# Attention times values as twenty block products, with half of the turned blocks going through DRAM

## The chip, the cores and the metric

The kernel runs on one core of one Trainium2 chip. The metric is the device time of one execution in microseconds; less is better. Everything is float32. A matmul in float32 is two TensorE instructions in the profile (a transpose on TensorE is one).

Names: PE is TensorE's matmul, PEld its weight load, DVE is VectorE, ACT ScalarE, POOL GpSimd, SP SyncE, which issues nearly all DMAs from one queue in order. Every engine runs its own instructions strictly in order; an instruction that waits holds up all behind it on that engine.

## The reference, cut to what matters

```python
B, L, S, D = 8, 100, 361, 512        # batches, queries, keys, width
H, K, F = 16, 128, 2048              # heads, width of a head, width of the MLP

def layer0(x, ctx):                  # one head, width 512, residual with factor alpha
    q, k, v = x @ wq.T, ctx @ wk.T, ctx @ wv.T
    return x + alpha * (softmax(q @ k.T / sqrt(512)) @ v) @ wo.T

def cross_attention(h, ctx):         # run twice, with weights of their own
    qh = (h @ wq + bq).reshape(B, L, H, K)
    kh = concat((ctx @ wk + bk).reshape(B, S, H, K), bias_k)   # one more key
    vh = concat((ctx @ wv + bv).reshape(B, S, H, K), bias_v)   # one more value
    p = softmax(einsum('bqhk,bthk->bhqt', qh, kh) / sqrt(K))
    return einsum('bhqt,bthk->bqhk', p, vh).reshape(B, L, H * K) @ wo + bo

x = layer0(x, ctx)
x = x + cross_attention(layer_norm(x), ctx)   # layer 1 of the two large ones
x = x + cross_attention(layer_norm(x), ctx)   # layer 2
x = x + gelu(layer_norm(x) @ w_fc1 + b_fc1) @ w_fc2 + b_fc2
```

## The kernel before, in words

The kernel never forms keys or values. A head's query is multiplied by `wk` transposed (the "wide query", 512 numbers), so that scores are wide query times context, and the probabilities are multiplied with the raw context first (the "mix", again 512 numbers per head and query) and with `wv` afterwards. Wide queries and mixes live in one tile `Z` of [128, 4, 2, 1600]: 4 chunks of the width 512, 2 batches, 16 x 100 rows (head, query).

The two attention layers are walked in steps (layer l, pair of batches q, head group g), 2 x 4 x 3 = 24 of them, each with two batches j: 48 tiles. `ROWS` gives the rows of a head group: 576, 512 and 512. They are scored in pairs of 128-row tiles (`PAIRS`), and in group 0 in one tile of 64 rows besides (`lone_tile`, `LONE`). For a pair:

- `pair_sums` (GpSimd) and `pair_part` form the scores in four parts by a product scheme with seven block products in place of eight (x, y, z in PSUM, evicted by ScalarE and VectorE); `pair_exps` and `normalise` make probabilities `p` of [128 rows, 361 keys and one bias key].
- `rows_turned` and `turned` put keys on partitions: VectorE transposes 32x32 blocks (L359). One instruction takes 32 rows x 192 numbers, for one quarter of the keys: 16 instructions for a pair of tiles, 8 smaller ones for the lone tile. They are placed 30 places behind in the scheduler's priority (`TURN_BEHIND`).
- the result is `pT`, a tile of nine blocks of [128, 288 or 256]: three key chunks (128, 128, 105 and the bias key) times two halves of the columns, and three places for sums. After the last quarter `column_sums` sends the bias key's row to DRAM (`pbd`) and forms four sums on GpSimd (L822 to L825).
- `mixed` (L843 on) multiplies the context's blocks with these: for each of two halves m of the width, four parts with 11 products of [128 or 105] x 128 x [288 or 256], accumulated in PSUM with evictions in between (L867, L870, L875 and L889 on ScalarE; L878, L884 and L885 on VectorE). Its result overwrites the tile's columns of `Z`. A next product into the same accumulation must wait for the eviction of the last.

The context's blocks come by `fill_ctx` in five loads per batch: three from the input, two from `cxd`, a DRAM tile that `ctx_sums` filled in layer 0 with five sums per batch (GpSimd, L442 to L446).

The order is written out by hand: the mix of a tile runs beside the scoring of the next tile, among the projections of the next step (`queries`, `wide_queries`) and the output products of the last one (`head_out`); `woven` and `apart` mix these lists, and `apart` keeps units with the same `chunks_of` from standing next to each other. A scheduler then orders instructions on each engine. Weights come by SP into rings of buffers (`W_SLOTS` 6, `V_SLOTS` 2, `C_SLOTS` 2 for the context); a load waits on SP until its buffer is free. PSUM has eight buffers for all uses.

Layer 0 comes first, one batch after the other: transposed context (`ctx_transposed`), scores, probabilities, mix, `ctx_sums`, output. Batches alternate between two rings for the raw context (`ctx0`, and `ctx` of [128, 2560]).

Of the kernel before, what the change touches and what calls it, by code (L numbers as in the profile page):

```python
# [19 lines left out]
P = 128  # L20
# [3 lines left out]
QB = 2  # L24
# [8 lines left out]
PAIRS = ((64, 320), (576, 832), (1088, 1344))  # L33
# [3 lines left out]
GWIDTH = 576  # L37

# [5 lines left out]
A11, A12, A22, A13, A23, A33, M1, M2, M3, M4 = range(10)  # L44
# [36 lines left out]
def two_cross_attentions(ctx: ExitStack, tc: tile.TileContext, a: dict, out: bass.AP):  # L81
# [16 lines left out]
    cxd = [dram.tile([P, 10 * P], F32, tag=f"cxd{b}", name=f"cxd{b}") for b in range(B)]  # L98
# [60 lines left out]
    def fill_ctx0(key, t):  # L159
        src = a["ctx_2048"][key[2]]  # L160
        t = t[:, : 3 * D].rearrange("p (k n) -> p k n", k=3)
        nc.sync.dma_start(out=t[:, :2, :], in_=src[: 2 * P].rearrange("(c p) n -> p c n", p=P))
        nc.sync.dma_start(out=t[:TS, 2, :], in_=src[2 * P :])

    def fill_ctx(key, t):
        if key[1] < 0:
            return fill_ctx0(key, t)
        src = a["ctx_2048"][key[2]]
        t = t.rearrange("p (m u n) -> p m u n", m=2, n=P)
        nc.sync.dma_start(out=t[:, :, A11, :], in_=src[:P].rearrange("p (m n) -> p m n", m=2)[:, :, :P])  # L170
        nc.sync.dma_start(
            out=t[:, :, A12:A13, :], in_=src[P : 2 * P].rearrange("p (m u n) -> p m u n", m=2, n=P)
        )
        nc.sync.dma_start(
            out=t[:TS, :, A13:A33, :], in_=src[2 * P :].rearrange("p (m u n) -> p m u n", m=2, n=P)
        )
        d = cxd[key[2]].rearrange("p (m u n) -> p m u n", m=2, n=P)
        nc.sync.dma_start(out=t[:, :, M1:, :], in_=d[:, :, 1:, :])
        nc.sync.dma_start(out=t[:TS, :, A33, :], in_=d[:TS, :, 0, :])
# [165 lines left out]
    def transposed(name, p, rows, dst):  # L345
# [4 lines left out]
        evacuate(dst, pt[:, :, :rows])  # L350

    def turned(p, dst, tiles, rows, quarter):

        keys = slice(quarter * QD, (quarter + 1) * QD)
        src = p[:, :tiles, :].rearrange("p m (k j b) -> p m k j b", k=3, b=QD)
        dst = dst.rearrange("p k (m i a) -> p m k i a", m=tiles, a=QD)
        with tc.high_priority(offset=-TURN_BEHIND):
            for i in range(rows // QD):
                nc.vector.transpose(dst[keys, :, :, i, :], src[i * QD : (i + 1) * QD, :, :, quarter, :])  # L359


# [76 lines left out]
    def ctx_sums(b):  # L438

        cx = ctx0(b).rearrange("p k (m u n) -> p k m u n", m=2, n=P)  # L440
        t = work.tile([P, 2, 5, P], F32, tag="pb", name=f"msum_{b}", bufs=1)
        nc.gpsimd.tensor_tensor(t[:, :, 1], cx[:, 0, :, 1], cx[:, 1, :, 1], ALU.add)  # L442
        nc.gpsimd.tensor_tensor(t[:, :, 2], t[:, :, 1], cx[:, 0, :, 0], ALU.subtract)
        nc.gpsimd.tensor_tensor(t[:, :, 3], cx[:, 0, :, 1], cx[:, 0, :, 0], ALU.subtract)
        nc.gpsimd.tensor_tensor(t[:, :, 4], cx[:, 1, :, 0], t[:, :, 2], ALU.subtract)
        nc.gpsimd.tensor_tensor(t[:TS, :, 0], cx[:TS, 2, :, 0], cx[:TS, 2, :, 1], ALU.subtract)  # L446
        out = cxd[b].rearrange("p (m u n) -> p m u n", m=2, n=P)
        tc.keep_in_program_order(nc.sync.dma_start(out=out[:, :, 1:, :], in_=t[:, :, 1:, :]))
        nc.sync.dma_start(out=out[:TS, :, 0, :], in_=t[:TS, :, 0, :])
# [78 lines left out]
    def layer0_units():  # L528
# [21 lines left out]
        for b in range(B):  # L550
            res.append(unit(lambda b=b: l0_probs(b)))
            res += scored(b + 1)
            res.append(unit(lambda b=b: l0_mixed(b), key0("ctx", b)))
            res.append(unit(lambda b=b: ctx_sums(b), key0("ctx", b)))
            res += turned(b + 2) + normed0(b + 1)
            res += weights(b + 4)
            if b == 0:
# [866 lines left out]
```

## Time and profile before

| what | us |
|---|---|
| median of three runs (lowest, highest) | 1986.92 (1986.24, 1991.32) |
| the profiled execution, its own time | 1987.13 |
| its span in the trace | 1985.3 |
| TensorE matmuls busy | 1942.6 |
| VectorE busy | 1279.1 |
| ScalarE busy | 761.3 |
| GpSimd busy | 699.8 |
| VectorE's transposes L359, 1664 of them | 602.2 |
| TensorE's mix L858, 2112 instructions | mean 391 (x), 390 (z), 388 (y) ns each |
| granted TensorE clock | 0.998 |

A span is what lies between the first and the last instruction in the trace; the execution's own time has the launch around it. The busy time of a group counts the time in which at least one of its instructions was under way; matmuls overlap each other, so the mean of one is longer than the distance between two. "Idle before" is the time that an engine stood still just ahead of a group, with what ended it. A wait on an engine that is not needed at that moment costs nothing.

### The profile page before, as it was taken

How to read it: one execution, taken by the hardware profiler on the slowest of the kernel's cores; microseconds unless marked ns; L12 is line 12 of the kernel's file. 1: busy time of each engine (PE TensorE's matmuls, PEld its weight loads, DVE VectorE, ACT ScalarE, POOL GpSimd, SP SyncE). 2: the span in 40 equal slices, each digit the busy share in tenths (PEclk: the TensorE clock that was granted, in tenths of full speed). 3: DMA queues.
4: the chain of work that ended last, by engine and by line, in shares of the span. 5: the costliest groups of instructions: out<-in, count | busy, mean ns of one | idle time of the engine just before them, and what ended most of it. 6: DMA issues, size and time to landing. Idle time of an engine off the chain costs nothing.

```text
span 1985.3 us, 31528 instructions
## 1 busy us (share of the span) xinstructions
PE 1942.6 (98%) x10991; PEld 1788.5 (90%) x10991; DVE 1279.1 (64%) x3555; ACT 761.3 (38%) x2018; POOL 699.8 (35%) x1147
## 2 busy tenths in 40 slices
PE   9999999999999999999999999999999999999999
PEld 5668899999999899999989898999999999889998
DVE  2464776667677677676765766676667677765553
ACT  0324544444442344344433344444433444421331
POOL 3232433543344144525243323333243243325140
PEclk9999999999999999999999999999999999999999
DMA  7696323742545356616533453234234442136432
GB/s 256 243 314 219 99 83 118 243 138 67 189 159 168 108 144 224 206 55 188 173 109 127 120 176 108 86 89 169 89 122 132 128 131 81 58 87 192 125 122 76
DMA packets 250683, 283.90 MB, mean 143 GB/s; under 512 B 37608, under 2 KB 212108, under 8 KB 247196
## 3 DMA queue, kind: packets, MB, share of 16 engines
q1 hardware_dynamic: 246340, 271.51, 43.1%
q0 software_dynamic: 2112, 6.40, 0.9%
q10 hardware_dynamic: 2072, 3.97, 0.6%
q8 instruction: 88, 1.44, 0.3%
q14 instruction: 71, 0.58, 0.1%
HBM read 242.86 MB, written 38.97 MB: 142 GB/s over the span
## 4 chain that ended last, share of the span: by engine, by line
PE 83%; DVE 10%; ACT 3%; DMA 2%; issue 1%; POOL 0%; SPq 0%; DVEq 0%; ACTq 0%
PE sx L748 10%; PE mx L858 9%; PE pq L672 8%; PE mz L858 7%; PE pwo_P L971 7%; PE po L908 7%; PE pqw L688 7%; DVE pT L359 5%; PE sz L748 5%; PE my L858 4%; PE sy L748 2%; PE pgx L1062 2%; PE pfx L1111 2%; PE pfz L1111 1%; PE pgz L1062 1%
## 5 line engine op out<-in xcount | busy, mean ns | idle before, releaser
L359 DVE STREAM_TRANSPOSE pT<-p 32x192 f32<-32x192 f32 (+1 forms) x1664 | 602.2, 362 | 90.9 <-ACT p L343 63.2
L858 PE MATMUL mx<-pT,ctx 128*128 128x256 f32 (+3 forms) x960 | 280.1, 391 | 8.2 <-DVE Z L884 3.1
L748 PE MATMUL sx<-cT,Z 128*128 128x181 f32 x1152 | 225.7, 317 | 2.1 <-DVE p L788 2.1
L782 POOL TENSOR_SCALAR p<-nsb 128x1 f32<-128x1 f32 x192 | 38.1, 217 | 499.1 <-DVE pT L359 441.2
L858 PE MATMUL mz<-pT,ctx 105*128 105x256 f32 (+3 forms) x768 | 206.1, 390 | 7.5 <-ACT Z L870 4.1
L748 PEld LDWEIGHTS sx<-cT,Z 128*128 128x128 f32 x1152 | 193.2, 190 | 13.7 <-DVE p L788 3.6
L672 PE MATMUL pq<-hT,wq 128*128 128x200 f32 x1024 | 194.5, 335 | 2.2 <-DMA wq<-in_L_xattn_wq_dram 2.2
L688 PE MATMUL pqw<-q,wkT 128*128 128x200 f32 x1024 | 194.4, 333 | 0.6 <-ACT q L680 0.6
L908 PE MATMUL po<-Z,wv 128*128 128x200 f32 x1024 | 194.8, 335 | 0.0
L858 PEld LDWEIGHTS mx<-pT,ctx 128*128 128x128 f32 (+1 forms) x960 | 169.4, 189 | 24.9 <-DVE Z L884 7.1
L802 ACT ACTIVATE p<-p,nm 128x362 f32<-128x362 f32 x192 | 114.7, 597 | 179.9 <-DVE nm L801 176.6
L672 PEld LDWEIGHTS pq<-hT,wq 128*128 128x128 f32 x1024 | 177.3, 191 | 6.9 <-issue 3.2
L688 PEld LDWEIGHTS pqw<-q,wkT 128*128 128x128 f32 x1024 | 176.2, 189 | 7.1 <-ACT q L680 1.4
L908 PEld LDWEIGHTS po<-Z,wv 128*128 128x128 f32 x1024 | 176.2, 191 | 5.0 <-issue 1.0
L858 PEld LDWEIGHTS mz<-pT,ctx 128*128 128x128 f32 (+1 forms) x768 | 144.2, 190 | 40.2 <-ACT Z L870 8.2
L801 DVE TENSOR_REDUCE nm<-p 128x1 f32<-128x362 f32 x192 | 101.5, 529 | 112.4 <-ACT p L793 102.7
L731 POOL TENSOR_TENSOR sums<-Z 128x256 f32<-128x256 f32 x96 | 70.8, 737 | 229.7 <-ACT Z L691 135.5
L691 ACT COPY Z<-pqw 128x400 f32<-128x400 f32 x256 | 122.4, 489 | 73.8 <-PE pqw L688 73.3
L748 PE MATMUL sz<-cT,sums 128*128 128x181 f32 x768 | 149.5, 316 | 0.0
L343 ACT ACTIVATE p<-p,rden 128x362 f32<-128x362 f32 (+2 forms) x216 | 129.0, 598 | 34.6 <-DVE rden L342 34.5
L748 PEld LDWEIGHTS sz<-cT,sums 128*128 128x128 f32 x768 | 124.7, 189 | 0.1
L858 PE MATMUL my<-pT,ctx 128*128 128x256 f32 (+3 forms) x384 | 102.6, 388 | 0.0
(385 smaller groups left out, 3095.5 us busy)
## 6 DMA issues: line engine op xcount, KB each, us to landing
wv<-in_L_xattn_wv_dram SPq DMA_DIRECT2D x64, 512.0 KB
wq<-in_L_xattn_wq_dram SPq DMA_DIRECT2D x64, 512.0 KB
wkT<-wkd SPq DMA_DIRECT2D x48, 512.0 KB
cT<-cTd SPq DMA_DIRECT2D x16, 1267.0 KB
wo_S<-wod SPq DMA_DIRECT2D x32, 512.0 KB
f<-in_L_xattn_w_fc_dram SPq DMA_DIRECT2D x32, 512.0 KB
wo_A<-in_L_xattn_wo_dram SPq DMA_DIRECT2D x24, 512.0 KB
xr<-xd SPq DMA_DIRECT2D x45, 200.0 KB
```

The costliest lines, as they stand in the source:

```text
L343: nc.scalar.mul(p[:rows, :n], p[:rows, :n], rden[:rows])
L359: nc.vector.transpose(dst[keys, :, :, i, :], src[i * QD : (i + 1) * QD, :, :, quarter, :])
L672: nc.tensor.matmul(ps, w[:, c, (h % 2) * K : (h % 2 + 1) * K], hTs[l, q][:, c, :], start=(c == 0), stop=(c == DT - 1),)
L688: nc.tensor.matmul(ps[:, c, :], w[:, h % 2, cc * P : (cc + 1) * P], qs[h], start=True, stop=True)
L691: nc.scalar.copy(Z[:, 2 * c2 : 2 * c2 + 2, :, h * L : (h + 1) * L], ps.rearrange("p c (b t) -> p c b t", b=QB),)
L731: nc.gpsimd.tensor_tensor(t[:, 0], a2[:, :2, :], a2[:, 2:, :], ALU.add)
L748: nc.tensor.matmul(ps[:, :KH], st["a"][a][:, c, :], st["ct"][:, blk, c, :], start=(first and c == 0), stop=(c == 1), skip_group_check=not ...
L801: nc.vector.tensor_reduce(nm, p[:, :S1], AX.X, ALU.max, negate=True)
L802: nc.scalar.activation(p[:, :S1], p[:, :S1], AF.Exp, bias=nm, accum_out=den)
L858: nc.tensor.matmul(ps, cx[:w, blk, :], pT[:w, u, :], start=first, stop=last, skip_group_check=more)
L908: nc.tensor.matmul(ps, w[:, c, (h % 2) * K : (h % 2 + 1) * K], Z[:, c, :, h * L : (h + 1) * L], start=(c == 0), stop=(c == DT - 1),)
L971: nc.tensor.matmul(ps, w[:, h, :], OB[i, j][:, h, :], start=(h == 0 and not more), stop=(h == 7), skip_group_check=more)
```

## The change

The mix of a tile becomes one product scheme over 4 x 3 x 2 blocks (four chunks of the width, three key chunks, two column halves): 20 products for both halves m together, in ten parts of two (`MIX`), one product for each of two accumulations ("lanes"). All contract over 128 partitions; the last key chunk is padded with zeros. Each product names the results to which its running sum is added, with a sign: 22 evictions, of which the first into each of the eight results goes by ScalarE (a copy, or a multiplication by -1) and the other 14 by VectorE.

The scheme needs twelve sums of the turned blocks (`TURN_SUMS`, six on VectorE, then six on GpSimd), which also use the tile's columns of `Z` as room, and twenty blocks of the context, 18 of them sums, from 23 additions (`CTX_SUMS`) of 128x128: 15 on GpSimd, eight on VectorE, held in the order of the program. All twenty blocks are written to `cxd` in four DMAs, and `fill_ctx` is one load of them.

The first pair of each tile is turned otherwise: `turned` is one transpose of all 128 partitions per quarter, 4 for the pair, which leaves every 32x32 block in its own partitions; `crossed` writes that to a DRAM tile and reads it back with the blocks on the right partitions, in 4 reads (head groups 1 and 2) or 8 (group 0). The second pair goes by `straight`, 16 transposes as before. In group 0 the lone tile moves from the first 64 rows to rows 256 to 319, and `PAIRS` and the loads of the score's bias (`nsb`) with it. The bias row goes to `pbd` in pieces. In layer 0 `bias_vectors` moves ahead of the first `ctx_sums`.

```diff
-PAIRS = ((64, 320), (576, 832), (1088, 1344))
+PAIRS = ((0, 320), (576, 832), (1088, 1344))
+LONE_AT = 2 * P
-A11, A12, A22, A13, A23, A33, M1, M2, M3, M4 = range(10)
+CTX_SUMS = (
+    (12, 1, 4, 1, 10),
+    (13, 1, 6, 1, 12),
...
+    (29, 1, 8, -1, 6),
+)
+CTX_ALSO = (4, 5)
+CTX_POOL = 15
+TURN_SUMS = (
+    (0, 9, 5, 1, "-"),
+    (0, 15, 2, 0, "-"),
+    (0, 7, 1, 0, "-"),
+    (0, 10, 7, 2, "+"),
+    (0, 8, 3, 10, "-"),
+    (0, 12, 8, 9, "-"),
+    (1, 14, 5, 3, "-"),
...
+    (1, 0, 2, 13, "-"),
+)
+MIX = (
+    (
+        (0, True, 4, 9, ((7, 1),)),
+        (1, True, 5, 15, ((0, 1),)),
+    ),
+    (
+        (0, True, 0, 15, ((6, 1),)),
+        (1, False, 6, 10, ((1, 1),)),
+    ),
+    (
+        (0, False, 1, 12, ((7, 1),)),
+        (1, False, 16, 1, ((7, 1),)),
+    ),
...
+    (
+        (0, True, 15, 4, ((2, 1), (3, 1))),
+        (1, False, 18, 8, ((3, 1), (5, 1))),
+    ),
+)
     def fill_ctx0(key, t):
...
+        nc.vector.memset(t[96:, 2, :], 0.0)
         nc.sync.dma_start(out=t[:, :2, :], in_=src[: 2 * P].rearrange("(c p) n -> p c n", p=P))
-        nc.sync.dma_start(out=t[:TS, 2, :], in_=src[2 * P :])
+        nc.sync.dma_start(out=t[:96, 2, :], in_=src[2 * P : 2 * P + 96])
+        nc.sync.dma_start(out=t[96:TS, 2, :], in_=src[2 * P + 96 :])
     def fill_ctx(key, t):
...
+        nc.sync.dma_start(out=t, in_=cxd[key[2]])
-    def turned(p, dst, tiles, rows, quarter):
+    def turned(p, dst, quarter):
+        src = p.rearrange("p m (k j b) -> p m k j b", k=3, b=QD)[:, :, :, quarter, :]
+        with tc.high_priority(offset=-TURN_BEHIND):
+            nc.vector.transpose(dst[:, quarter], src)
+    def straight(p, dst, quarter):
         keys = slice(quarter * QD, (quarter + 1) * QD)
...
+            for i in range(P // QD):
+                nc.vector.transpose(dst[keys, :, i], src[i * QD : (i + 1) * QD])
+    def crossed(name, src, dst, whole):
+        d = dram.tile([P, 4 * 6 * QD], F32, tag=f"turn{count[0] % 4}", name=f"turn_{name}")
+        nc.sync.dma_start(out=d, in_=src)
+        d = d.rearrange("(i k) (j m n) -> j k i m n", k=QD, j=4, m=2)
+        for j in range(4):
+            for x, y in [(dst, d)] if whole else [(dst[:, :, m], d[:, :, :, m]) for m in range(2)]:
+                nc.sync.dma_start(out=x[j * QD : (j + 1) * QD], in_=y[j])
     def ctx_sums(b):
...
+        for n, (i, f, x, g, y) in enumerate(CTX_SUMS):
+            x, y = (x, y) if f == 1 else (y, x)
+            engine = nc.gpsimd if n < CTX_POOL else nc.vector
+            ins = engine.tensor_tensor(block(i), block(x), block(y), ALU.add if f == g else ALU.subtract)
+            if n >= CTX_POOL:
+                tc.keep_in_program_order(ins)
+        out = cxd[b].rearrange("p (u n) -> p u n", n=P)
+        nc.sync.dma_start(out=out[:, 8:18, :], in_=more)
+        nc.sync.dma_start(out=cxd[b][:, : 8 * P], in_=t[:, 12 * P : 20 * P])
+        for k, i in enumerate(CTX_ALSO):
+            nc.sync.dma_start(out=out[:, 18 + k, :], in_=block(i))
+    def slots(l, q, g, j):
+        t, more = turned_tile(l, q, g, j)
+        n = more.shape[1] // 3
+        res = [t[:, h, ..., k, :] if g == 0 else t[:, h, :, :, k] for k in range(3) for h in range(2)]
+        res += [blocks(more[:, u * n : (u + 1) * n], g) for u in range(3)]
+        return res + [blocks(Z[:, m, j, r : r + n], g) for m in range(DT) for r in (ROWS[g][0], ROWS[g][0] + n)]
-    def column_sums(l, q, g, j, engine=nc.gpsimd):
+    def column_sums(l, q, g, j):
+        t = slots(l, q, g, j)
+        row = pbd[l, q * QB + j][:, slice(*ROWS[g])].rearrange("o (h x) -> o h x", h=2)
+        for h in range(2):
+            x, y = blocks(row[:, h], g), t[4 + h][TS : TS + 1]
+            for x, y in [(x, y)] if g == 0 else [(x[:, m], y[:, m]) for m in range(2)]:
+                nc.sync.dma_start(out=x, in_=y)
+        for e, i, x, y, sign in TURN_SUMS:
+            (nc.vector, nc.gpsimd)[e].tensor_tensor(t[i], t[x], t[y], ALU.add if sign == "+" else ALU.subtract)
     def rows_turned(l, q, g, j, r, quarter):
...
+        p, h = probs[l, q, j, r][0], PAIRS[g].index(r)
+        t, more = pair_tile(l, q, g, j, h)
+        if h:
+            straight(p, t, quarter)
+        else:
+            turned(p, more.rearrange("p (j m k a) -> p j m k a", j=4, m=2, k=3), quarter)
+        if quarter == 3:
+            if not h:
+                crossed(f"{l}_{q}_{g}_{j}_{h}", more, t.rearrange("p m i k a -> p i m (k a)"), g > 0)
+            if h:
+                column_sums(l, q, g, j)
-    def mixed(l, q, g, j, m, part):
...
+    def mixed(l, q, g, j, part):
+        cx = rings["ctx"].tiles["ctx", l, q * QB + j].rearrange("p (u n) -> p u n", n=P)
+        t = slots(l, q, g, j)
+        h = (ROWS[g][1] - ROWS[g][0]) // 2
+        for lane, opens, u, v, results in MIX[part]:
+            if opens:
+                ps = psum(ps_mm, [P, h], f"m{'xz'[lane]}_{l}_{q}_{g}_{j}_{part}")
+                lanes[lane] = blocks(ps, g)
+            ps = lanes[lane]
+            nc.tensor.matmul(ps, cx[:, u, :], t[v], start=opens, stop=True, skip_group_check=True)
+            for o, f in results:
+                key, dst = (l, q, g, j, o), t[9 + o]
+                if key not in begun:
+                    begun.add(key)
+                    nc.scalar.mul(dst, ps, float(f)) if f != 1 else nc.scalar.copy(dst, ps)
+                elif abs(f) == 1:
+                    nc.vector.tensor_tensor(dst, dst, ps, ALU.add if f == 1 else ALU.subtract)
...
-        return fn.args[4] if isinstance(fn, partial) and fn.func is mixed else None
+        return fn.args[:4] if isinstance(fn, partial) and fn.func is mixed else None
```

## The prediction

> **What bounds the kernel now.** I read the busy times and the chain first, then one stretch of TensorE in order of time, then the waits in front of weight loads, then what could slow the engines that the change loads.
>
> ```profile
> span 1985.3 us, 31528 instructions
> PE 1942.6 (98%) x10991; PEld 1788.5 (90%) x10991; DVE 1279.1 (64%) x3555; ACT 761.3 (38%) x2018; POOL 699.8 (35%) x1147
> ...
> PE 83%; DVE 10%; ACT 3%; DMA 2%; issue 1%; POOL 0%; SPq 0%; DVEq 0%; ACTq 0%
> ```
>
> TensorE is busy in 98% of the span, and 83% of the chain that ended last lies on it. Time can come from nothing but less TensorE work, and be lost by anything that makes TensorE wait. What a matmul really costs is read from the timeline of TensorE, since the busy time of a group also counts pipeline ends that overlap the next group:
>
> ```profile
> 899.76 1.03 PE L858 MATMUL mz<-pT,ctx 128*128 128x256 f32 x4
> 900.63 0.78 PE L748 MATMUL sx<-cT,Z 128*128 128x181 f32 x4
> ```
>
> Four matmuls of 256 columns start at 899.76 and the next group at 900.63: 0.217 us each, 0.85 ns a column, though a single one is listed with 383 ns. Over all 10,991 instructions (columns x 0.846 ns) that gives 1923 us, so only 62 us of the span are not matmul streaming. In 300 to 1700 us TensorE is busy 1386.4 of 1400 us; there is hardly a wait to remove. VectorE has 953.3 us there (68%), GpSimd 517.6 (37%).
>
> The waits in front of the mix (weight loads, since they wait first):
>
> ```profile
> PEld mz L858 <- ACT Z L870: 8.2, 11, 1.0
> PEld mx L858 <- DVE Z L884: 7.1, 13, 1.4
> ...
> PEld mz L858 <- POOL pT L822: 5.7, 7, 2.1
> ```
>
> Columns are total us, times, longest. The next product into the same accumulation waits for the eviction of the last; 7.1 us fall on 96 such steps through VectorE (0.074 each). With L867 (3.7) and L875 (2.9) ScalarE's 288 steps cost 14.8 us (0.051 each).
>
> **The change, part by part.**
>
> *Products.* A tile (layer, pair of batches, head group, batch; 48 of them) had 22 products, now 20; each is two matmul instructions. 192 instructions go: 128 of 256 columns (0.217 us) and 64 of 288 (0.244): 27.7 + 15.6 = 43.3 us, all on the path. Contraction over 128 instead of 105 rows costs nothing (379 ns with 105 rows, 383 with 128). The moving operand now comes in runs of 32 numbers; the nearest row, L908 with runs of 100, has the same 335 ns as the contiguous L672, so I take no loss.
>
> *Evictions.* ScalarE keeps 8 per tile. VectorE goes from 6 to 14: 256 more of 256 columns (0.418 us) and 128 of 288 (0.452), +165 us.
>
> *Turning.* The second pair keeps 16 transposes of 32x192. The first pair has 4 of 128x192 instead of 16 of 32x192: 576 fewer instructions.
>
> ```profile
> L359 DVE STREAM_TRANSPOSE pT<-p 32x192 f32<-32x192 f32 x1536 | 567.8, 370 | 79.8 <-ACT p L343 55.3 <-POOL sums L733 1.4
> ```
>
> No row has 128 partitions. The bounds are one row (0.37 us) and four rows (1.48 us); I take 0.37, as a pass over 361 columns takes 528 ns on 100 partitions (L332) and 529 on 128 (L801). -213 us, or nothing saved at the other end.
>
> *Column sums.* GpSimd's 4 per tile (0.73 and 0.79 us) become 6, +74 us for it; VectorE gets 6 new ones with both inputs in SBUF. Alone these cost about 0.42 us (0.28 at 128 columns, L604; 0.57 at 400, L1020). Beside GpSimd they do not:
>
> ```profile
> 98.63 0.78 DVE L467 TENSOR_TENSOR cT_-1_4_632<-cT_-1_4_632 128x362 f32<-128x362 f32 x1
> 99.45 0.95 DVE L468 TENSOR_TENSOR cT_-1_4_632<-cT_-1_4_632 128x362 f32<-128x362 f32 x1
> 100.32 1.05 DVE L469 TENSOR_TENSOR cT_-1_4_632<-cT_-1_4_632 128x362 f32<-128x362 f32 x1
> ...
> 98.99 1.02 POOL L443 TENSOR_TENSOR msum<-msum,ctx_-1_3_230 128x256 f32<-128x256 f32 x1
> 99.96 1.02 POOL L446 TENSOR_TENSOR msum<-ctx_-1_3_230 105x256 f32<-105x256 f32 x1
> ```
>
> The same three take 0.53 to 0.54 with GpSimd idle. Transposes (0.37) and evictions from PSUM (0.43) are equal in both cases. With GpSimd busy about 40% I take 0.58 to 0.61 for each: +170 us.
> [...]
>
> VectorE's sum per tile: 8 x 0.43 + 6 x 0.59 - 12 x 0.37 = +2.5 us. From 68% of a 32.3 us tile (22.0) it goes to 24.5 of 31.4 us, 78%: it does not become the bound, but is later in its queue.
>
> *Waits in the mix.* By MIX, 240 steps now go through VectorE and 336 through ScalarE: at the rates above 17.8 + 17.1 = 35 us of weight-load idle against 21.9. Between a product and the next into the same accumulation lie, in the order of the changed program, a median of 1.8 us of other matmuls (2.2 before). Bounds: -11 us (the matmuls' own idle behind these evictions, all gone) and +30 (VectorE's rate doubled, weight-load idle passed on in full). I take +6, as about half of such idle reached the matmuls before.
>
> *The way through DRAM.* Per tile SP issues one write of 384 KB behind the fourth transpose, and 4 reads of 96 KB (8 of 48 KB in the first head group) behind that write. The sum "15" on VectorE reads what they bring, so here a VectorE instruction waits for a DMA; behind it in its queue stand the second pair's transposes and evictions, for which the mix waits. Nearest rows: four loads of 128 KB, used as soon as landed,
>
> ```profile
> 811.14 1.90 SPq L139 DMA_DIRECT2D wor<-in_L_xattn_wo_dram  x4
> ...
> 814.93 0.72 POOL L936 TENSOR_TENSOR wor<-wor 128x256 f32<-128x256 f32 x1 [5.83 <-DMA wor<-in_L_xattn_wo_dram]
> ```
>
> 3.8 us, up to 5.0 elsewhere; and a read behind its own write: SP waits 1.5 us on average for pbd (2 KB), up to 2.8 for xd (200 KB), and 3.9 us passed for cxd's 512 KB. With 0.4 us for the issue: 5.7 to 9.3 us, I take 7.6. Against it stands what VectorE has to do between the fourth transpose and that sum, in the changed program's order: 2.9 to 3.8 us in 7 tiles, 5.1 to 6.2 in 12, more in 29; at 75% busy 4.7 and 7.5 us pass. So VectorE stops for 7 x 2.9 = 20 us. Bounds: nothing, and 62 us (the rival below). I take half, +10, the rest falling into VectorE's spare 22%.
> [...]
>
> *SP's queue.* 392 more issues at 0.45 us, 176 us. SP already waits 203.1 us behind transposes (L821), and TensorE waited 2.2 us in all for a weight load; the six weight buffers cover it. Were that cover gone, each late load would cost a wait like that 2.2 us. The mix's context comes in one load instead of five, with the same bytes. Traffic grows by 38 MB of turned blocks and 5 MB of context blocks on 284 MB; nothing on TensorE waits for bandwidth.
>
> *Layer 0.* Per batch GpSimd goes from 5 sums (3.6 us) to 15 (0.47 each, L705: 7.1 us), 8 of them early, while GpSimd stood idle from 27 to 65 us; VectorE gets 8 in the order of the program (0.28 alone, 0.53 beside GpSimd: 2.2 to 4.2 us). It is 67% busy there (33.54 of 50 us), 7 of some 10.4 us a batch; 9.2 to 11.2 after. Behind these sums wait the next transposed context and the scores. Bounds 0 and 26 us (eight batches at 3.2, the middle of the two, all on the path); I take 6 batches x 1.2 = +7.
>
> **Sum**, against the profiled execution's own 1987.13 us (span 1985.3 and 1.8 around it; the median shown is 1986.92, the same within 0.2): -43.3 + 6 + 10 + 7 = -20, **1967 us**.
>
> **Rivals.**
> - *The turned blocks come late* (the other side). The round trip takes 9.3 us, and SP's reads stand behind a weight load that waits for its buffer: such loads stand between write and last read in 27 of 48 tiles, and SP's waits behind L908 average 4.2 us (206.7 over 49). VectorE stops 7 x 4.6 + 12 x 1.8 = 54 us and some 17 x 4.2 = 71 more; half reaches TensorE, 62 us: 1987 - 43 + 6 + 7 + 62 = 2019. It decides from 30 us on, 0.6 us a tile. For: the sums stand close behind the transposes. Against: in most tiles there is room.
> - *The evictions eat the gain.* VectorE's steps at double rate, +30 instead of +6: 1991. For: 240 steps for 96, at 78%. Against: no step has less than 0.7 us of other matmuls to wait under.
> - *All of it is covered.* Waits as before: 1944. For: 22% spare on VectorE.
> - *A 128-row transpose is four.* VectorE keeps 213 us and is 92% busy; a third of it reaching TensorE gives 2038. Against: L332 and L801 above.
>
> **How the numbers follow.** Forecast 0.43, its own range 1950 to 1982; late blocks 0.24; evictions 0.14; all covered 0.12; transposes 0.07. A measurement of this kernel tells 0.3% (6 us) from no change, so faster is below 1981: 0.39 of the forecast, 0.12, 0.03 of the evictions and 0.02 of late blocks, 0.56. Same: 0.04 + 0.08 + 0.02 = 0.14. Slower 0.30. The range runs from the covered case to the late blocks, 1944 to 2015; above lie part of these and the transposes.
>
> **What would show it.** 10,799 matmuls, with some 1880 us of streaming. 128x192 transposes near 0.37 us; the 288 sums near 0.6. VectorE waiting at the column sums for the turn loads: about 20 us is my case, over 100 the rival. Waits of mx and mz behind VectorE about 18 us. Matmul idle in 50 to 200 us up by about 7. The prediction is wrong if TensorE's idle time outside these three places grows, above all for weights behind SP.

## The result: 88 us slower

The changed kernel takes 2075.11 us (median; 2066.82 to 2080.70) where the kernel before takes 1987.12: a ratio of 1.0432, with a 95% interval of 1.0409 to 1.0454. The forecast was 1967. The profiled execution lasted 2074.14 us (span 2072.1), so it is a typical one. The head of its page:

```profile
span 2072.1 us, 32542 instructions
PE 1940.2 (94%) x10799; PEld 1768.8 (85%) x10799; DVE 1395.3 (67%) x3723; ACT 754.6 (36%) x2018; POOL 841.6 (41%) x1323
```

192 matmul instructions are gone, as forecast, and yet TensorE is busy almost as long as before (1942.6) and its idle time has grown from 42.7 to 131.9 us. To see what a busy time hides I used the same measure as the prediction: the time from the start of one group of matmuls to the start of the next, less columns x 0.846 ns. I call what is left *loss*. It was 53 us and is 183 now, 130 more; 130 - 43 (streaming saved) = 87, the whole difference of the two spans. By what stands behind the lost time:

| kernel | us | loss | to 200 us | before mix products | before score products | rest |
|---|---|---|---|---|---|---|
| before | 1987.1 | 53 | 22 | 23 | 12 | -4 |
| changed | 2075.1 | 183 | 42 | 75 | 42 | 23 |

(The rest is negative because of the lone tile's scores, 256 matmul instructions of 181 columns on 64 rows: they start in pairs, two some 7 ns apart and the next pair some 150 ns later, where the measure takes 153 ns for each. That is some 15 us less than the measure in the kernel before. Matmuls of 200 columns follow each other every 169.0 ns, 169.2 by the measure.) So 110 of the 130 us were lost behind 200 us, in the attention and not in layer 0, and they were lost in front of the mix *and* of the scores and the other products, which the change does not touch.

How that looks in one tile: VectorE of the changed kernel in order of time.

```profile
912.26 0.42 DVE L952 TENSOR_TENSOR Z<-pT 128x256 f32<-128x256 f32 x1 [2.67 <-DMA pT<-turn]
...
917.06 3.84 DVE L443 STREAM_TRANSPOSE pT<-p 32x192 f32<-32x192 f32 x10
920.93 0.43 DVE L1035 SCALAR_TENSOR_TENSOR O<-po,vecs,pb 128x200 f32<-128x200 f32 x1
921.27 0.91 DVE L952 TENSOR_TENSOR Z<-pT 128x256 f32<-128x256 f32 x1
922.10 0.94 DVE L952 TENSOR_TENSOR pT<-pT 128x256 f32<-128x256 f32 x1
922.97 0.33 DVE L888 TENSOR_TENSOR p<-sz,p 128x180 f32<-128x180 f32 x1
923.22 0.69 DVE L952 TENSOR_TENSOR Z<-pT 128x256 f32<-128x256 f32 x1
...
924.17 0.60 DVE L952 TENSOR_TENSOR pT<-pT,Z 128x256 f32<-128x256 f32 x1
924.70 0.33 DVE L893 TENSOR_TENSOR p<-sx,p 128x180 f32<-128x180 f32 x1
```

The sum "15" waits 2.67 us for the turn loads, then the second pair's transposes run, and only behind the last of them, at 920.90, can the other sums begin. They take 0.6 to 0.94 us each. Between them stand L888 (behind two of them) and L893 (behind four), which empty the accumulators of the *scores* of the next tile. GpSimd meanwhile runs its own sums, and TensorE:

```profile
919.33 0.78 PE L853 MATMUL sy<-cT,Z 128*128 128x181 f32 x4
922.32 0.67 PE L1000 MATMUL mx<-Z,ctx 128*128 128x256 f32 x2 [2.21 <-DVE Z L952]
922.83 0.59 PE L1000 MATMUL mz<-Z,ctx 128*128 128x256 f32 x2
925.09 1.57 PE L853 MATMUL sx<-cT,Z 128*128 128x181 f32 x4 [1.67 <-DVE p L893]
926.46 1.06 PE L1000 MATMUL mx<-Z,ctx 128*128 128x256 f32 x2
927.31 1.06 PE L1000 MATMUL mz<-Z,ctx 128*128 128x256 f32 x2
```

Two waits, 2.21 us for the sum and 1.67 us for L893. (Ahead of these rows, at 915.0, TensorE had waited 1.49 us for an eviction, L1007, that stood behind the sum "15" and four transposes. How far a waiting instruction holds up those behind it shows there too: the L1007 that starts at 912.60 empties a product that had ended at 909.96, while VectorE stood idle to 912.26.) And a further loss that no wait shows: from 925 on a pair of 256 columns takes 0.85 us from start to start instead of 0.43 to 0.51. The granted clock has fallen (0.50 from 924.2 to 930.8 us, 1.00 before and after).

Waits (the ends of groups to the next starts) grew from 33 to 122 us in the whole kernel, 89 of the 130. The clock stood at half for 71.7 us in all, 11.2 before; by an estimate (half of TensorE's busy time there) that cost 29 us against 3. Most of the rest are the ends of matmuls in front of a wait, which a next group otherwise overlaps (24 us against 11).

In the kernel before, TensorE's own waits for sums and at the scores were small (total us, times, longest):

```profile
PE sx L748 <- ACT p L773: 4.3, 6, 2.2
...
PE mz L858 <- POOL pT L822: 3.4, 4, 1.6
...
PE sx L748 <- DVE p L788: 2.1, 3, 0.8
```

Those of the changed kernel: weight loads and matmuls at the mix, matmuls at the scores, and two that explain them:

```profile
PEld mz L1000 <- ACT Z L1005: 26.2, 31, 2.2
...
PEld mx L1000 <- DVE Z L952: 11.3, 6, 3.3
PEld mx L1000 <- DVE Z L1007: 9.1, 12, 1.5
...
PE mx L1000 <- DVE Z L952: 24.0, 17, 3.1
PE mz L1000 <- ACT Z L1005: 15.4, 12, 1.7
...
PE sx L853 <- ACT p L884: 9.9, 6, 3.3
PE sx L853 <- DVE p L893: 8.4, 7, 1.7
...
ACT Z L1005 <- DVE Z L952: 31.7, 16, 3.4
...
DVE Z L952 <- DMA pT<-turn: 6.0, 4, 2.7
```

VectorE stops for the turn loads 6.0 us in all; the rival of late blocks needed over 100. Behind VectorE's evictions (L1007) weight loads of mx wait 9.1 us, where 7.1 stood before, and those of mz another 2.5; for both together some 18 were forecast. What TensorE waits for are the sums (L952) and what comes behind them. ScalarE's L1005 comes behind them too: it waits 31.7 us for VectorE's sums, because it writes over a block of Z that the last of them still reads, and L884, for which the scores wait 9.9 us, runs on the same engine. (Another 19.6 us stand in front of weight loads of mx with no wait that the profile shows; without VectorE's sums they are 4.0.) (The chain that ended last, 83% TensorE before, can be followed only through some 20% of the span here, and is of no help.) Over all tiles the distance tells the same: the last of the four sums ended 3.2 us (median) after the last transpose before (the 2.45 in two expectations below is where the third ended), now VectorE's end 4.6 and GpSimd's 6.9 us after it, while the mix's first product starts 2.3 us after it (4.8 before). The costs themselves:

```profile
L435 DVE STREAM_TRANSPOSE pT<-p 128x192 f32<-128x192 f32 x192 | 59.0, 350 | 17.1 <-ACT p L421 16.1 <-POOL pb L1025 0.6 <-DMA sbd<-sT 0.2
L952 DVE TENSOR_TENSOR Z<-pT 128x256 f32<-128x256 f32 x96 | 57.8, 602 | 7.0 <-DMA pT<-turn 6.0
...
L952 DVE TENSOR_TENSOR pT<-pT 128x256 f32<-128x256 f32 x32 | 29.9, 934 | 0.0
L952 DVE TENSOR_TENSOR pT<-pT,Z 128x256 f32<-128x256 f32 x32 | 22.1, 690 | 0.3
```

The 128-partition transpose takes 0.35 us. VectorE's eight groups of sums add up to 212 us (0.74 each), GpSimd's to 254 us.

### The profile page after: what moved, and what is told of

The parts are those of the page before. It is cut to its first block, busy times and chain, and to the rows that moved or that the text cites. A ratio compares the mean times of both kernels' runs of the same rounds, so it can differ in the third digit from the quotient of the medians.

```text
span 2072.1 us, 32542 instructions
## 1 busy us (share of the span) xinstructions
PE 1940.2 (94%) x10799; PEld 1768.8 (85%) x10799; DVE 1395.3 (67%) x3723; ACT 754.6 (36%) x2018; POOL 841.6 (41%) x1323
## 5 line engine op out<-in xcount | busy, mean ns | idle before, releaser
L443 DVE STREAM_TRANSPOSE pT<-p 32x192 f32<-32x192 f32 x768 | 283.8, 370 | 25.3 <-ACT p L421 13.0
L853 PE MATMUL sx<-cT,Z 128*128 128x181 f32 x1152 | 232.1, 322 | 18.5 <-ACT p L884 9.9
L1000 PE MATMUL mz<-pT,ctx 128*128 128x256 f32 (+1 forms) x672 | 205.4, 392 | 4.6 <-ACT Z L1005 4.4
L1007 DVE TENSOR_TENSOR Z<-Z,mx 128x256 f32<-128x256 f32 (+1 forms) x384 | 155.2, 422 | 48.7 <-PE mx L1000 46.5
L1000 PE MATMUL mx<-Z,ctx 128*128 128x256 f32 (+1 forms) x480 | 155.5, 407 | 28.8 <-DVE Z L952 24.0
L952 POOL TENSOR_TENSOR Z<-pT 128x256 f32<-128x256 f32 (+1 forms) x144 | 132.2, 931 | 52.6 <-DVE pT L443 48.3
L1000 PE MATMUL mx<-pT,ctx 128*128 128x256 f32 (+1 forms) x480 | 148.5, 391 | 4.9 <-DVE Z L1007 4.9
L1000 PEld LDWEIGHTS mz<-pT,ctx 128*128 128x128 f32 x672 | 125.6, 190 | 32.2 <-ACT Z L1005 8.2
L1007 DVE TENSOR_TENSOR Z<-Z,mz 128x256 f32<-128x256 f32 (+1 forms) x288 | 119.7, 426 | 36.7 <-PE mz L1000 32.9
L1005 ACT COPY Z<-mx 128x256 f32<-128x256 f32 (+1 forms) x192 | 72.9, 380 | 191.6 <-PE mx L1000 190.5
```

The costliest lines, as they stand in the source:

```text
L443: nc.vector.transpose(dst[keys, :, i], src[i * QD : (i + 1) * QD])
L853: nc.tensor.matmul(ps[:, :KH], st["a"][a][:, c, :], st["ct"][:, blk, c, :], start=(first and c == 0), stop=(c == 1), skip_group_check=not ...
L952: (nc.vector, nc.gpsimd)[e].tensor_tensor(t[i], t[x], t[y], ALU.add if sign == "+" else ALU.subtract)
L1000: nc.tensor.matmul(ps, cx[:, u, :], t[v], start=opens, stop=True, skip_group_check=True)
L1007: nc.vector.tensor_tensor(dst, dst, ps, ALU.add if f == 1 else ALU.subtract)
```

## The experiments

All times are medians of timed runs; the kernel before, run beside them, stood at 1988.6 (1989.5 with the last two). In the diffs `-` is the changed kernel unless said otherwise.

### One part left out at a time

**All twelve column sums out.**

```
-        for e, i, x, y, sign in TURN_SUMS:
+        for e, i, x, y, sign in ():
...
-            nc.tensor.matmul(ps, cx[:, u, :], t[v], ...)
+            nc.tensor.matmul(ps, cx[:, u, :], t[v % 6], ...)
```

> The changed kernel with the twelve column sums of each tile left out (six on VectorE, six on GpSimd); a product whose input was a sum reads one of the six turned blocks instead, so it waits for transposes and turn loads but for no sum. Theory A (the mix's products now stand behind sums that run on VectorE and GpSimd after the last transpose, and TensorE has nothing else left to do there): of the 88 us lost against the kernel before, most comes back, 60 to 95 us, 1980 to 2015 us, and TensorE's waits at the mix for Z behind VectorE's sums (24 us) and the slow clock that follows them go. Theory B (the eight extra VectorE evictions of a tile, which stay): under 30 us come back, 2045 to 2075. Theory C (layer 0's context sums): nothing beyond 5 us.

Measured: 1974.99 us, ratio to before 0.9931 (0.9914 to 0.9949). 100 us come back, and both the mix (loss 75 to 32) and the scores (42 to 15) recover, though all 14 evictions a tile are still on VectorE. The loss after 200 us is 40 us, where the kernel before has 31 and the changed one 141. So the extra evictions cost at most 9 us here, and nearly the whole loss of the attention is the sums'. Whether as work or as something to wait for is not yet told.

**Only VectorE's six out.**

```
-        for e, i, x, y, sign in TURN_SUMS:
+        for e, i, x, y, sign in TURN_SUMS[6:]:
```

with the products that read those six reading turned blocks.

> The changed kernel with only VectorE's six column sums of each tile left out; the products that read them read turned blocks instead, GpSimd's six stay. Theory A in the form that VectorE's sums (212 us of its time, and the first two products wait for them) set the end: nearly as much as without all twelve comes back, 45 to 85 us, 1990 to 2030. In the form that GpSimd's six (254 us, 0.85 to 1.09 each where they meet VectorE) set it: under 30 us, 2045 or more, and the mix waits for GpSimd instead. Theory B: under 25 us.

Measured: 2040.23 us. 35 come back, between the two forms. The waits for scores are nearly gone (loss 18; 12 before, 42 changed), but the mix now waits for GpSimd:

```profile
PE mx L1000 <- POOL pT L952: 45.5, 22, 4.8
```

Each engine's sums hide part of what the other's cost: 65 us are left without VectorE's six.

**The way through DRAM out.**

```
-            turned(p, more.rearrange("p (j m k a) -> p j m k a", j=4, m=2, k=3), quarter)
+            turned(p, t.rearrange("p m i k a -> p i m k a"), quarter)
...
-            if not h:
-                crossed(...)
```

> The changed kernel without the way through DRAM: the first pair's four 128x192 transposes write into the turned tile directly (so those blocks hold other numbers than the reference's), and the write and the four or eight reads of each tile are gone. The prediction's term for this was 10 us, its rival 62. The trace shows VectorE waiting 6.0 us for turn loads in all, so by Theory A 5 to 15 us come back (2060 to 2070); if the queue of SP behind these 392 issues and its waits (168 us for the transposes, 73 for the write) is what delays TensorE through late loads, 30 to 70 us come back, 2005 to 2045.

Measured: 2058.55 us, 17 less: a little more than the first range, far from the second. The queue of SP behind 392 more issues is not what takes most of the 88 us. How the 17 divide between late loads, as in the tile above, and the issues was not measured.

**Layer 0's context sums out.**

```
-        for n, (i, f, x, g, y) in enumerate(CTX_SUMS):
+        for n, (i, f, x, g, y) in enumerate(()):
```

> The changed kernel with layer 0's 23 context sums per batch left out (15 on GpSimd, 8 on VectorE); what is written to the context store is the plain blocks, with the same bytes. TensorE's losses up to 300 us grew from 23 to 55 us. Theory C (these sums hold up VectorE's order in layer 0 and with it the scores and transposes): 15 to 30 us come back, 2045 to 2060. If the padded context load, the way to the store and its reading back are what grew, under 8 us: 2067 or more. After 300 us the losses should stay what they were (about 110 us).

Measured: 2060.34 us, 15 less: the small end of theory C (the profiled executions differ by 11). The loss before 200 us falls from 42 to 32, not to the 22 of the kernel before. One thing that stays is a weight load that is late at the start of the attention; its issue stands behind the context's stores and readings in the queue of SP (changed kernel, queue of SP, then the wait on TensorE):

```profile
168.86 0.32 SPq L257 DMA_DIRECT2D ctx<-cxd  x1
...
184.65 0.59 SPq L244 DMA_DIRECT2D wkr<-in_L_xattn_wk_dram  x1
```

```profile
PE pwk L766 <- DMA wkr<-in_L_xattn_wk_dram: 4.9, 1, 4.9
```

Without the context sums TensorE still waits 6.9 us there.

### Work or waiting?

**The sums run, nobody reads them.** All twelve stay on their engines, writing three spare blocks; the products read blocks that no sum writes.

```
-        for e, i, x, y, sign in TURN_SUMS:
+        for e, i, x, y, sign in SPARE_SUMS:
...
-            nc.tensor.matmul(ps, cx[:, u, :], t[v], ...)
+            nc.tensor.matmul(ps, cx[:, u, :], t[v % 4 + 1], ...)
```

> The changed kernel with all twelve column sums of each tile still run on the same engines with the same shapes, but into the three spare blocks of the turned tile, and no product reads them: the mix reads turned blocks that no sum writes (the output is not the reference's). Without the sums the time was 1975. Theory L (latency: TensorE loses because the products wait until the sums are done, some 4.6 us on VectorE and 6.9 on GpSimd after the last transpose against 2.45 before): 1975 to 1995, TensorE's waits for L952's results gone. Theory W (work: what costs is that VectorE and GpSimd are held by the sums, so that scores' and products' evictions come late): 2030 to 2070, as all the work is still there.

Measured: 2095.45 us, above both ranges and even 20 more than the changed kernel. Theory L, which I then favoured, falls for the sums as a whole: no product waits for a sum here, and the time is still lost, in front of the scores (loss 65, against 15 with no sums), the mix (66 against 32) and the rest (31 against -7). Why it is slower than the changed kernel, where the sums are read, is not shown.

**The mix begun two units later.**

```
+                lead = min(lead + 2, len(part))
                 fill += part[:lead]
```

> The changed kernel, computing the reference, with the first product of every mix put two units of other TensorE work later (a unit is a head's query or output product, some 1.4 to 2.7 us of matmuls; where fewer are left, all of them). Theory L: the products find more sums done, 20 to 55 us come back, 2020 to 2055. Theory W: the engines' work is the same, no change, 2065 to 2085.

Measured: 2117.27 us, 42 more, outside both ranges. TensorE hardly waits for the sums now, but longer for the evictions of the mix (16.8 us at mx for L1007, 7.8 in the changed kernel; 25.7 at mz for L1005, 15.4) and for L893 (19.6, 8.4): products that come later stand closer together, and VectorE is late for them.

**All twelve on VectorE.**

```
-            (nc.vector, nc.gpsimd)[e].tensor_tensor(t[i], t[x], t[y], ...)
+            nc.vector.tensor_tensor(t[i], t[x], t[y], ...)
```

> The changed kernel, computing the reference, with all twelve column sums on VectorE, in the order of the list. VectorE gets some 125 us more work, but no sum meets another on GpSimd, so 0.42 to 0.46 each instead of 0.6 to 0.9 on VectorE and 0.85 to 1.09 on GpSimd: the last ends some 5.5 to 6 us after the last transpose instead of 6.9, the first ones sooner. Theory L: 5 to 35 us come back, 2040 to 2070. Theory W: VectorE is more loaded, 2085 to 2120.

Measured: 2121.69 us, 47 more, as theory W has it (just above its range), although half of the sums now take no more than some 0.43 us (mean 0.53).

**The kernel before with nine sums for four** (here `-` is the kernel before).

```
-        engine.tensor_tensor(t[:, 6], t[:, 1], t[:, 0], ALU.subtract)
+        for _ in range(3):
+            engine.tensor_tensor(t[:, 6], t[:, 1], t[:, 0], ALU.subtract)
...
```

> The kernel before, computing the reference, with its four column sums per tile on GpSimd made nine by running three of them again (three, three, one and two times): the last is done some 6.5 us after the last transpose instead of 2.45, as in the changed kernel; VectorE has no more to do, and GpSimd (35% busy) some 190 us more. Theory L: TensorE waits as in the changed kernel, 30 to 90 us slower, 2020 to 2080. Theory W: GpSimd is far from full and VectorE is untouched, 1987 to 2000.

Measured: 2040.68 us, ratio 1.0261 (1.0243 to 1.0279): 52 us lost in the *old* kernel by five more sums on an engine that is 43% busy with them. The last sum ends 8.7 us (median) after the last transpose, later than the 6.9 of the changed kernel. Here it is waiting (L823 and L825 are sums that run three times):

```profile
PE mx L861 <- POOL pT L825: 24.9, 16, 2.4
PE mz L861 <- POOL pT L823: 19.4, 11, 3.1
```

The scores lose next to nothing (loss 14, 12 before). So both theories are right: GpSimd's sums are waited for, VectorE's stand in the way. VectorE's are waited for too (24.0 us at mx in the changed kernel); what that is worth alone, no run here tells.

### The two engines apart

In the next two, one half of the unread sums is left out too (`SPARE_SUMS[:6]`, `SPARE_SUMS[6:]`).

> As the kernel whose twelve sums are run but not read (2095), with GpSimd's six left out: only VectorE's six are run, nobody waits for their results. Without any sums the time was 1975. Theory V (VectorE's sums cost as work: they stand ahead of the additions that empty the score products' accumulators, L893, and these came on average 1.5 to 1.6 us after their product with the sums against 0.6 without): 2015 to 2050, score waits of TensorE some 30 us or more as in the changed kernel. Theory G (what cost in that kernel were GpSimd's six, by its own order and by slowing VectorE): 1975 to 1995.

Measured: 2033.50 us, in the range of theory V.

> The counterpart: only GpSimd's six sums are run, not read by any product. Theory V: 1975 to 1995, since GpSimd is 40% busy and nothing on TensorE's path stands right behind its sums; the 65 us between no sums (1975) and GpSimd's six read (2040) are then all waiting for their results. Theory G: 2030 to 2070.

Measured: 1972.25 us, just under the range of theory V and the same as with no sums at all (1974.99).

This settles it. As work, GpSimd's six alone cost nothing; read, they cost 2040 - 1975 = 65 us. VectorE's six cost 58 us (2033.5 - 1975) with nobody waiting for them. How late VectorE then comes to the scores can be measured directly: L893 starts, after the end of its product, on average 0.5 us in the kernel before, 1.5 in the changed one, 0.6 with no sums, 0.6 with GpSimd's alone, 1.4 with VectorE's alone and 1.6 with both. The scores are not all of it: of the 61 us more loss than with no sums, 20 stand in front of the scores, 21 of the mix and 20 of other products. TensorE with no sums, then with VectorE's alone (psb waits for hT, which VectorE also empties from an accumulator):

```profile
PE mx L1000 <- DVE Z L1007: 7.9, 8, 2.4
...
PE sx L853 <- DVE p L893: 4.1, 3, 2.1
...
PE psb L743 <- DVE hT L687: 3.0, 2, 1.7
```

```profile
PE sx L867 <- DVE p L907: 18.1, 10, 3.2
PE mx L1014 <- DVE Z L1021: 10.7, 8, 3.1
PE psb L757 <- DVE hT L701: 9.2, 7, 2.6
```

And together, unread, they cost 120 us, 62 more than their sum. The groups show why. VectorE's alone:

```profile
L966 DVE TENSOR_TENSOR pT<-pT 128x256 f32<-128x256 f32 x192 | 98.5, 552 | 0.8
```

The same sums with GpSimd's beside them:

```profile
L966 POOL TENSOR_TENSOR pT<-pT 128x256 f32<-128x256 f32 x192 | 153.5, 799 | 50.6 <-DVE pT L457 40.1 <-DMA wkT<-wkd 0.4
L966 DVE TENSOR_TENSOR pT<-pT 128x256 f32<-128x256 f32 x192 | 144.1, 789 | 0.5
```

0.55 us grow to 0.79, just where VectorE is needed most; the last section follows single sums.

**Ten on GpSimd, two on VectorE.** Four entries of `TURN_SUMS` ("7", "10", "8", "12") change from engine 0 to 1.

> The changed kernel, computing the reference, with four more of the sums on GpSimd: VectorE keeps the two that the first two products read, GpSimd has ten, in the order of the list. VectorE has 2.8 us less to do a tile just ahead of the scores' additions, GpSimd's last sum ends some 8 us after the last transpose instead of 6.9. If VectorE's place is what weighs most: 2040 to 2060. If waiting for the results weighs most: 2080 to 2110. Both at once, cancelling: within 10 us of 2075.

Measured: 2083.10 us: the two effects cancel, as the third case had it. Score losses fall from 42 to 21, mix losses rise from 75 to 126.

**All three parts out.**

> The changed kernel with column sums, the way through DRAM and layer 0's context sums all left out, as in the three single kernels (1975, 2059, 2060): what is left are the 192 fewer matmul instructions, the eight more VectorE evictions a tile and layer 0's reordered stores and loads. By the prediction's term for the streaming (43.3 us) and nothing for the evictions: 1944 plus 7 to 15 us for layer 0's weights that come late behind its stores, 1948 to 1962. If the moving operand in runs of 32 numbers or the evictions cost anything, 1970 or more.

Measured: 1955.59 us. It is in the forecast range: 1988.6 - 43.3 and 12 us more loss than the kernel before (65 against 53) make 1958, so the streaming term is confirmed. Operands in runs of 32 numbers and eight more evictions can cost no more than these 12 us here (8 of them at the mix, 31 against 23).

### Can it be mended?

In the kernel with ten on GpSimd the largest wait of TensorE was not for a sum:

```profile
PE mz L1000 <- ACT Z L1005: 56.3, 31, 4.9
...
ACT Z L1005 <- POOL Z L952: 85.8, 31, 5.7
```

ScalarE's eviction of the second product writes the block of Z that holds the sum "9", and GpSimd's sum "12" has still to read it. I tried to free that block (slot 16 for slot 9):

```
-    (0, 9, 5, 1, "-"),
+    (0, 16, 5, 1, "-"),
...
-        (0, True, 4, 9, ((7, 1),)),
+        (0, True, 4, 16, ((7, 1),)),
```

> The kernel with ten sums on GpSimd (2083), computing the reference, with one difference: the sum "9" is kept in the eighth block of Z (slot 16) instead of the first (slot 9), so that the mix's second product can be evicted into the first block without waiting until GpSimd has read "9" for its sum "12"; the eviction into the eighth block now waits for that, and no product stands behind it. Theory S (that wait is most of it): ScalarE's 85.8 us of waits for GpSimd and TensorE's 64 us at mz go, 2005 to 2040. Theory R (waiting for the results themselves): 2065 to 2090.

Measured: 2098.43 us, worse by 15 and above both ranges. It did not test what it was meant to: the eviction into slot 16 stands *ahead* of the other in ScalarE's queue, so the wait came earlier and grew to 173.5 us. The three that build on it:

> As d1_spare_slot, computing the reference, with all twelve sums on GpSimd, none on VectorE. GpSimd's last sum ends some 9 us after the last transpose, but the products need them one after another over some 20 us. Theory S: 1990 to 2030, less than d1 since VectorE has nothing in front of the score additions. Theory R: 2060 to 2100, as all twelve are later.

Measured: 2110.01 us, 10 above the range of theory R, and far from theory S.

> As d2_all_gpsimd, computing the reference, with the mix begun one unit of other TensorE work (1.4 to 2.7 us) later. If first products still wait for GpSimd's sums there: 10 to 30 us less than d2. If the mix's later products get too dense for their evictions, as two units later did with the changed kernel (2117): 5 to 30 us more than d2.

Measured: 2073.27 us, 37 less, more than forecast: with VectorE freed of the sums, beginning the mix one unit later does help, where with the changed kernel two units had done harm.

> As d1_spare_slot, computing the reference, with all 23 context sums of a batch in layer 0 on GpSimd instead of 15 (8 on VectorE, in program order). Leaving all 23 out gave 15 us. If VectorE's eight are what costs: 7 to 15 us less than d1. If GpSimd's, by slowing VectorE's 128x128 scalings from 0.28 to 0.53 us beside it: up to 10 us more than d1.

Measured: 2104.17 us, no better than d1 (its loss up to 200 us is 50 against 42): layer 0's sums cost no less on GpSimd alone.

Last, all twelve on GpSimd (engine 1), the reader "12" moved up to the fifth place with slot 9 as in the changed kernel, and the mix two or three units later:

```
-    (0, 9, 5, 1, "-"),
-    (0, 15, 2, 0, "-"),
+    (1, 9, 5, 1, "-"),
...
+    (1, 12, 8, 9, "-"),
+    (1, 15, 2, 0, "-"),
...
+                lead = min(lead + 2, len(part))
```

> The changed kernel, computing the reference, with all twelve sums on GpSimd, "12" (the last reader of the first product's operand) moved up to the fifth place, and the mix begun two units of TensorE work later. With one unit later (d3) 2073, of which some 90 us were TensorE's losses at the mix. If waiting for GpSimd's sums is what is left: 2010 to 2050. If the mix's products, closer together, wait for their evictions instead: 2065 to 2100.

Measured: 2025.96 us.

> As e1_gpsimd_two_later with the mix begun three units later. If waiting for sums is still what weighs: 10 to 40 us less than e1, and below the kernel before only if nearly all of the 90 us goes (under 1987). If density has taken over: 10 to 40 us more than e1.

Measured: 2022.24 us, ratio to before 1.0173 (1.0146 to 1.0199). ScalarE's wait for GpSimd is down to little:

```profile
ACT Z L1005 <- POOL Z L952: 7.9, 4, 4.6
```

The third unit gives no more than the second within the spread. Some 53 us of the 88 are mended, computing the same. Against the 43 us of streaming saved it still loses more than the kernel before: 36 us at the mix, 18 up to 200 us, 21 elsewhere. At the mix TensorE now waits for VectorE's evictions (L1007), 26.3 us at mx and mz, where 7.8 stood in the changed kernel: with the sums out of the way, what the rival of the evictions feared begins to show. No version here that computes the reference beats the kernel before, and with every sum free it would be 1975, with layer 0's and the way through DRAM free too, 1956. Which of the two edits (order, delay) did most from 2073 to 2026 was not separated.

## Why the prediction was wrong

- *Streaming, -43.3*: right; 1956 with the three suspects out.
- *Evictions, +6*: right in size. With the sums out the mix loses 9 us more than before (32 against 23) with 14 evictions a tile on VectorE. That rival falls for the changed kernel; in the last version, with the mix later, L1007 does hold TensorE up (26.3 us).
- *Turning, 0.37 us a transpose*: 0.35. The rival of four falls.
- *The way through DRAM, +10*: 17 by leaving it out. VectorE's own waits are 6.0 us (20 forecast); what the other 11 are is not shown. The rival of late blocks named the right sign and 32 of the 88 us, for a cause that is worth 17.
- *Layer 0, +7*: too small. The loss up to 200 us grew by 20, inside the bounds (0 to 26). VectorE was busy 43.1 of 50 us from 100 to 150 us (33.5 before):

```profile
100.00:150.00 50.00, 39.77 (x211) 27.81 (x208) 43.12 (x173) 11.64 (x39) 27.53 (x54) 0.93 0.80 285
```

  (Columns as in a table of stretches: width, busy us and instructions of TensorE, its weight loads, VectorE, ScalarE, GpSimd; clock, DMA share, GB/s.) Leaving the 23 sums out gave 10 of the 20 us back, and VectorE's eight were no cheaper on GpSimd; what the other 10 are stays open but for the next term. *SP's queue, 0*: here the cover was gone once, 4.9 us.
- *Column sums*: this is the step that failed. Their durations were mis-sized (0.74 us instead of 0.59 on VectorE; GpSimd's 254 us instead of 220, the 146 before and 74), but that is 42 and 34 us of engines with room. (Of the rows of the kernel before that the prediction shows for this, L468 and L469 end 0.39 us after the GpSimd sums that were under way when they started; the last section has such ends for this kernel.) The error was the sentence "From 68% of a 32.3 us tile (22.0) it goes to 24.5 of 31.4 us, 78%: it does not become the bound, but is later in its queue." No term of the sum followed from that "later", and none from the mix's waits for the sums themselves. In 300 to 1700 us VectorE is busy only 987 of 1400 us, 70%, less than I feared, and still it decides. Two prices were missing. First, all but one of VectorE's sums can start only behind the last transpose, and they stand there in one burst ahead of what VectorE empties for TensorE, the scores' additions, evictions of the mix and others: 58 us alone, and more beside GpSimd. Second, the mix's first products now read sums, where before the first one read a turned block; I asked what evictions wait for, and never how long after the last transpose the last sum ends: 3.2 us became 6.9, and reading GpSimd's six (6.6 us without VectorE's) is worth 65 us by itself. Both together, overlapping, are the 100 us that leaving out the sums gives back, of the 108 by which the forecast was low.
- *The clock* was in no term. Of the 130 us of added loss, some 25 are matmuls at the lower clock, by the estimate above.

## What to carry to other kernels

Ask of every instruction that is added to an engine with room *where* in its queue it stands: if it can only start at one point, and what the busiest engine waits for stands right behind, a mean of 70% hides nothing, and the sum needs a term for it. Where operands become results of further work, work out how long after the last input the last of them is ready, and compare it with the distance to the first reader. What nobody waits for can be free, but ask whom it slows: six sums a tile on GpSimd cost nothing unread, 65 us read, and 62 us unread beside VectorE's six, which cost 58 us alone though nobody read them.

## What was not expected of the hardware

**Short waits cost twice.** The granted clock of the changed kernel fell to half in 15 stretches, 11 of them between 205 and 1850 us (925.1 to 930.8 in the tile above lies in one), that of the kernel before in 3, one of them there. Most follow idle time of TensorE, often a single wait of some 2 to 3 us (1.93 ending at 1456, 2.52 at 1388, 3.06 at 525) or two close together (2.21 and 1.67 at 925). In the runs here the cost, estimated as above, grows with the waits: 6 us beside 52 of waits with no sums, 29 beside 122, 46 beside 141 with the mix two units later.

The traces of the two kernels show more. In each of them all changes of the clock lie on one grid with steps of 3.41 us. Stretches of this grid in the changed kernel (width, busy us and instructions of TensorE, clock, DMA share, GB/s):

```profile
1453.19:1456.60 3.41, 1.48 (x8) 1.00 0.87 281
1456.60:1460.01 3.41, 3.41 (x11) 0.50 0.12 40
1460.01:1463.42 3.41, 3.41 (x20) 1.00 0.00 0
```

1.93 us idle in one step, and the next is at half clock; busy all through that one, and the clock is back. In these two traces (from 20 us on, up to 8 us before the end) 1146 steps were at full clock. 13 of them had 2.05 us or more of idle time, and after every one of these the clock fell; of those with less than 1.78 us none was followed by a fall; of the six between, three were. Where a wait lay mattered too: one of 2.44 us that ended at 263.82 was shared by two steps, 0.54 and 1.90 us, and left the clock at 1.00.

**VectorE's sums end just behind GpSimd's instruction.** At 921 to 923 us VectorE's sums take 0.91 and 0.94 us while GpSimd's take

```profile
921.85 1.78 POOL L952 TENSOR_TENSOR Z<-pT 128x256 f32<-128x256 f32 x2
```

0.9 each (0.73 in the kernel before). 240 of VectorE's 288 sums start while an instruction of GpSimd is under way. 227 of these end 0.28 us (median; 0.28 to 0.32 for the middle 90%) after that instruction, which had 0.04 to 3.38 us left when they started. The other 13 end before it, in 0.41 to 0.45 us, and there it is GpSimd's instruction that takes long, 1.08 to 1.75 us. The 48 sums that meet none at their start take 0.43 us. Beside a long instruction it is plain:

```profile
1104.01 3.77 POOL L1069 TENSOR_TENSOR O<-O 128x1600 f32<-128x1600 f32 x1
...
1104.40 3.70 DVE L952 TENSOR_TENSOR Z<-pT,Z 128x288 f32<-128x288 f32 x1
```

Four sums took 3.1 to 3.7 us in this way, and two of TensorE's longest waits end some 2.4 us behind two of them (4.46 us to 1110.53, 6.11 us to 1535.13). The mean over all 288 is only 0.74 us: at the start of the 227 GpSimd's instruction had 0.44 us left (median).
